# Last stage of a two-layer kernel: three sequences chosen with the attention, one after it, ranks from sums of signs, rows gathered with addition

## The chip, the cores and the metric

The kernel runs on one core of a Trainium2 chip. A core has a matrix engine (TensorE, PE in the profile), a vector engine (VectorE, DVE), an engine for activations (ScalarE, ACT), a general one (GpSimd, POOL) and one that only issues transfers (SyncE, SP). Each works through its own list of instructions in order and waits on semaphores. Transfers (DMA) are issued from the queues of SP, ACT and POOL; gathers by a list of row numbers are issued by POOL. The metric is the device time of one execution in microseconds (us), the median of several runs. Before the change it is 2228.92 us, the median of 3 runs (2227.93 to 2233.76).

## What is computed

Four sequences of 1024 tokens with 256 features go through two layers. The first (windowed attention and a routed feed-forward) and the second layer's attention are untouched. The second feed-forward is a mixture in which each of 8 experts chooses its 128 tokens of each sequence:

```python
gate_logits = jnp.einsum('bnd,de->bne', x, gate_w)
competitive_gates = sinkhorn(gate_logits)      # 8 rounds: normalise over tokens, then over experts
vals, idx = jax.lax.top_k(jnp.swapaxes(competitive_gates, -1, -2), M)   # M = 1024 // 8 = 128
...
routed = x[b_idx, routed_indices]
outputs = jnp.einsum('ebmd,edf->ebmf', routed, experts) * gate_values
routed_back = jnp.zeros_like(x).at[b_idx, routed_indices].set(vals_bmed)
return routed_back                             # the layer adds this to x
```

(`routed` and `outputs` are shortened here.) A token that several experts choose keeps the result that is written last, that of the largest place among the 128 and, at equal places, of the largest expert number; a token that none chooses gets zero.

## The kernel before

A tile is 128 tokens; there are 32 tiles, 8 to a sequence. The residual stream lives in 32 tiles `x_t` in SBUF, 128x256 each.

**The second attention** is one loop of 256 steps (32 tiles `p` by 8 key blocks `k`). In a step PE makes the scores (`one<-q_st,k_st`), takes away the row maxima (`one<-top_st,minus`) and sums the values (`acc<-wide,v_t`); ACT makes the exponentials (L1870). The row maxima of the tile 12 steps ahead are made in the same loop: in each step DVE reduces one 128x1024 block (L1820) and two 128x512 blocks (L1823). For the last 12 steps there is nothing ahead any more, so these reductions end 12 steps before the loop does. When a tile's maxima are complete they go out to DRAM and come back as rows (`tops_d`, `top_st`, L1843 and L1848, on SP). Jobs beside the attention are generators in lists (`outs`, `projects`, `between`, `gating`, `sort`, `aside`), and `some()` takes a piece of each twice a step. `sort` goes on only where another job gave PE something to do, or when `idle` is set. During the attention PE's instructions are held in the order in which they are written.

**From attention to gates.** `put_out` (L1900 to L1926) makes a tile's attention output, `finish` normalises groups of tiles (on POOL, except for the last tile, on DVE), `gate_steps` normalises them again, writes them to DRAM (`xn_d`) and makes the gates. `share_steps` (L1316 to L1330) is the 8 rounds of normalising: a sum over tokens on PE and five small operations on DVE a round, each waiting for the one before.

**Choosing.** Sequences are taken in two groups of two (`GB = 2`). Group 0 is complete at tile 15. `choose_steps` sorts it during the attention: 16 rounds of MAX8 (the eight largest of each row, L1354), FIND_INDEX8 (their places, L1356) and MATCH_REPLACE8 (striking them out, L1360), over 16 rows (sequence and expert) of 1024. Group 1 is sorted after the attention by `choose_halves` in two parts of 8 rounds, with four FIND_INDEX8 at the end of a part (all at L1420), so that the first 64 tokens of each expert can be fetched while the rest are sorted.

**Experts.** `take_rows` (L1477) gathers an expert's token rows from `xn_d` with one POOL instruction for each. `experts_on` (group 0) and `half_experts` (group 1) transpose them on PE, multiply by the expert's weights, scale by the gate on ACT (L1516, L1553) and write to `y_d` on SP (L1520, L1558).

**Ranks and back.** For each token one needs the row of `y_d` that was to be written last, so the largest rank (place plus one, zero where an expert did not choose the token). Group 0: `ranks` scatters places into a DRAM table `rank_d` (16 indirect writes by POOL, L1993), and `read_ranks` reads it back on SP (L1615). Group 1: `ranks_of` makes, for each expert, a 128x1024 comparison of tokens with places (`hot`, by ACT as a sign in the first part at L2270, by DVE as an equality in the second at L2268), which PE sums into ranks. `sources` (L1570 to L1587) turns ranks into row numbers with 11 operations on DVE. `back` gathers the rows with POOL (L1596) into a tile `yr`, an engine adds `x_t` (L1602), and `put_taken` writes the sum to the output (L1609, SP).

The last two tiles' outputs, group 1's `share_steps`, sorting, experts and rows back all come after the attention, in this order; group 0's experts run beside group 1's sorting. A scheduler places the instructions of this part on their engines.

Of the kernel before, what the change touches and what calls it, by code (L numbers as in the profile page):

```python
# [39 lines left out]
def two_layers(  # L40
# [765 lines left out]
    GB = 2  # L806
    GE = GB * E
    TB = S // P
    GT = GB * TB
# [9 lines left out]
    first_slot = fpool.tile([P, 1, E], F32, name="first_slot")  # L819
    nc.vector.tensor_scalar(first_slot, expert_no, float(CAP), -1.0, ALU.mult, ALU.add)  # L820

    place1_i = fpool.tile([P, 1], I32, name="place1_i")
    nc.gpsimd.iota(place1_i, pattern=[[0, 1]], base=1, channel_multiplier=1)
    place1 = fpool.tile([P, 1], F32, name="place1")
    nc.vector.tensor_copy(place1, place1_i)
# [4 lines left out]
    y_d = [fdram.tile([E * CAP + 1, D], F32, name=f"y_d{b}") for b in range(NB)]  # L830

    rank_d = [fdram.tile([S * E, 1], F32, name=f"rank_d{b}") for b in range(GB)]
    none = fpool.tile([P, S * E // P], F32, name="none")
    nc.gpsimd.memset(none, 0.0)
    for b in range(GB):
        nc.gpsimd.dma_start(out=rank_d[b].rearrange("(p n) o -> p (n o)", p=P), in_=none)
    for b in range(NB):
        nc.gpsimd.dma_start(
            out=y_d[b][E * CAP :, :].rearrange("o (p n) -> (o p) n", p=4), in_=none[:4, :]
        )  # L840
# [468 lines left out]
    def share_steps(g: int, bank, lag: int):  # L1309


        mine = gates[:, g * GT : (g + 1) * GT, :]
        by_seq = mine.rearrange("p (b t) e -> p b t e", b=GB)
        for _ in range(8):
            part = small.tile([P, GB, E], F32, tag="part", name="part")
            nc.vector.tensor_reduce(part, by_seq.rearrange("p b t e -> p b e t"), AX.X, ALU.add)  # L1316
            for _ in range(lag):
                yield 0
            ps = bank()
            mm_on(  # L1320
                ps[:, :GE], lhsT=ones1, rhs=part.rearrange("p b e -> p (b e)"),
                start=True, stop=True,
            )
            rc = small.tile([P, GB, 1, E], F32, tag="rc", name="rc")
            nc.vector.reciprocal(rc[:, :, 0, :], ps[:, :GE].rearrange("p (b e) -> p b e", b=GB))
            nc.vector.tensor_tensor(by_seq, by_seq, rc.to_broadcast([P, GB, TB, E]), ALU.mult)
            rsum = small.tile([P, GT, 1], F32, tag="rsum", name="rsum")
            nc.vector.tensor_reduce(rsum[:, :, 0], mine, AX.X, ALU.add)
            nc.vector.reciprocal(rsum, rsum)
            nc.vector.tensor_tensor(mine, mine, rsum.to_broadcast([P, GT, E]), ALU.mult)  # L1330
            yield 1

    def choose_steps(g: int, bank, chosen, after):

        by_tile = gpool.tile([P, TB, GE], F32, tag="by_tile", name="by_tile", bufs=1)
        nc.vector.tensor_copy(
            by_tile.rearrange("p t (b e) -> p t b e", b=GB),
            gates[:, g * GT : (g + 1) * GT, :].rearrange("p (b t) e -> p t b e", b=GB),
        )
        yield 0  # L1340
        cur = gpool.tile([GE, S], F32, tag="cur", name="cur")
        for hf in range(2):
            ps = bank()
            for t in range(TB // 2):
                turn_on(
                    ps[:GE, t * P : (t + 1) * P], by_tile[:, hf * TB // 2 + t, :], ident
                )
            nc.vector.tensor_copy(cur[:, hf * 512 : (hf + 1) * 512], ps[:GE, :])
            yield 1
        top_v = gpool.tile([GE, CAP], F32, tag="top_v", name="top_v", bufs=1)  # L1350
        top_i = gpool.tile([GE, CAP], U32, tag="top_i", name="top_i", bufs=1)
        for k in range(CAP // 8):
            eight = slice(8 * k, 8 * k + 8)
            nc.vector.max(out=top_v[:, eight], in_=cur)  # L1354
            yield 0
            nc.vector.max_index(out=top_i[:, eight], in_max=top_v[:, eight], in_values=cur)  # L1356
            yield 0
            if k < CAP // 8 - 1:
                nxt = gpool.tile([GE, S], F32, tag="cur", name="cur")
                nc.vector.match_replace(  # L1360
                    out=nxt, in_to_replace=top_v[:, eight], in_values=cur, imm_value=-1.0
                )
                cur = nxt
                yield 0
        top_f = gpool.tile([GE, CAP], F32, tag="top_f", name="top_f", bufs=1)
        nc.vector.tensor_copy(top_f, top_i)
        ps = bank()
        turn_on(ps[:, :GE], top_v, ident[:GE, :GE])
        turn_on(ps[:, GE : 2 * GE], top_f, ident[:GE, :GE])
        slot_gate = gpool.tile([P, GE], F32, tag="slot_gate", name="slot_gate", bufs=1)  # L1370
        nc.vector.tensor_copy(slot_gate, ps[:, :GE])
        slot_tok = gpool.tile([P, GE], F32, tag="slot_tok", name="slot_tok", bufs=1)
        nc.vector.tensor_copy(slot_tok, ps[:, GE : 2 * GE])
        slot_row = gpool.tile([P, GE], I32, tag="slot_row", name="slot_row", bufs=1)
        nc.vector.tensor_copy(slot_row, slot_tok)
        chosen[g] = slot_gate, slot_tok, slot_row
        after()
        yield 1
# [3 lines left out]
    def choose_halves(g: int, bank, chosen, after, pool, parts: int = 2):  # L1382

        by_tile = pool.tile([P, TB, 2, GE], F32, tag="by_tile", name="by_tile", bufs=1)
        for n in range(2):
            nc.vector.tensor_copy(
                by_tile[:, :, n].rearrange("p t (b e) -> p t b e", b=GB),  # L1390
                gates[:, g * GT : (g + 1) * GT, :].rearrange("p (b t) e -> p t b e", b=GB),
            )
        yield 0
        cur = pool.tile([P, 4, S], F32, tag="cur", name="cur", bufs=1)
        for hf in range(2):
            ps = bank()
            for t in range(TB // 2):
                nc.tensor.transpose(
                    ps[:32, t * P : (t + 1) * P],
                    by_tile[:, hf * TB // 2 + t].rearrange("p n e -> p (n e)"),  # L1400
                    ident,
                )
# [19 lines left out]
        for k in range(rounds):  # L1422
# [23 lines left out]
            n = GE // parts  # L1446
            for k0, top in enumerate((top_v, top_f)):
                for j in range(part * 4 // parts, (part + 1) * 4 // parts):
                    q = slice(32 * j, 32 * j + 32)
                    for h in range(parts):  # L1450
                        row = 64 * h + 32 * (j % 2) if parts == 2 else 32 * j
                        with ExitStack() as order:
                            if part:
                                order.enter_context(tc.issue_after(newest["ranks"]))
                            mm(
                                ps[row : row + 32, k0 * n : (k0 + 1) * n],
                                lhsT=top[q].rearrange("p a i -> p (a i)"),
                                rhs=ident[q, 32 * j + h : 32 * j + GE : parts],
# [3 lines left out]
            slot_gate = pool.tile([P, n], F32, tag=f"slot_gate{part}", name="slot_gate", bufs=1)  # L1462
            slot_tok = pool.tile([P, n], F32, tag=f"slot_tok{part}", name="slot_tok", bufs=1)
            slot_row = pool.tile([P, n], I32, tag=f"slot_row{part}", name="slot_row", bufs=1)
# [7 lines left out]
    def take_rows(slots, columns, pool):  # L1472

        xgs = []
        for b, n in columns:
            xg = pool.tile([P, D], F32, tag="xg", name="xg", bufs=16)
# [20 lines left out]

    def experts_on(g: int, xgs, pool, w_all):

        slot_gate = chosen[g][0]  # L1500
# [865 lines left out]
```

## Time and profile before

The profiled execution took 2230.59 us; its span, from the first instruction to the last, is 2228.9 us. The stages that the change touches, by the span's clock:

| us | what runs | length | PE busy | DVE busy | POOL busy |
|---|---|---|---|---|---|
| 1303.9 to 1662.2 | attention, twelve tiles' maxima, no choosing beside it | 3 x 119.4 | 347.9 | 275.9 | 86.8 |
| 1662.2 to 1791.4 | the same, with group 0's normalising rounds | 129.2 | 123.6 | 103.8 | 28.9 |
| 1791.4 to 1922.2 | the same, with group 0's sorting | 130.8 | 123.3 | 122.1 | 25.3 |
| 1922.2 to 2038.5 | the last four tiles' maxima, rest of the sorting | 116.3 | 107.0 | 108.9 | 28.3 |
| 2038.5 to 2100.2 | last 12 steps, last tiles' outputs and gates | 61.7 | 48.0 | 15.2 | 39.8 |
| 2100.2 to 2125.5 | group 1's normalising rounds | 25.3 | 7.3 | 16.2 | 15.0 |
| 2125.5 to 2177.8 | group 1's sorting, group 0's experts and rows back | 52.3 | 35.9 | 50.1 | 30.2 |
| 2177.8 to 2228.9 | second half of group 1's experts, rows back, output | 51.1 | 17.5 | 20.1 | 30.4 |

"Busy" is the time in which an engine had an instruction in work. An idle engine costs nothing by itself: what counts is which chain of waits ends last.

### The profile page before, as it was taken

The numbers are of one execution on the slowest core, as the hardware profiler recorded it, in microseconds if no ns is written. First come the engines' busy times: TensorE is split into PE (matmuls) and PEld (weight loads), VectorE is DVE, ScalarE is ACT, GpSimd is POOL, SyncE is SP. The second block draws the span as 40 slices with busy tenths as digits, with TensorE's granted clock in tenths as the row PEclk, the third lists the DMA queues.
The fourth block names the chain that finished last, engine by engine and source line by source line (L and its number), as shares of the span: only waits on it lengthen the run. The fifth ranks groups of instructions, "written<-read, shape, count | busy, mean of one in ns | idle before, by whom it ended". The sixth has DMA issues, their size and how long they took to land.

```text
span 2228.9 us, 50307 instructions
## 1 busy us (share of the span) xinstructions
PE 2056.2 (92%) x19908; PEld 1345.7 (60%) x19908; DVE 1357.5 (61%) x2704; ACT 1002.5 (45%) x1916; POOL 653.0 (29%) x862
## 2 busy tenths in 40 slices
PE   6999989999999999998899999999999999998563
PEld 4777765655788888864455555555555555544341
DVE  6676654522222222244888777878777899996394
ACT  3555542111122222221266676767666566666331
POOL 3656541342000000022331222213131212115546
PEclk9999999999999999998999999999999999999676
DMA  5111105114167666734252313131313113100235
GB/s 148 53 47 47 49 13 202 48 64 139 43 212 236 225 228 210 238 119 108 75 118 52 71 50 77 50 78 50 68 37 82 40 38 70 50 21 12 79 101 171
DMA packets 207016, 212.77 MB, mean 95 GB/s; under 512 B 90024, under 2 KB 166088, under 8 KB 206780
## 3 DMA queue, kind: packets, MB, share of 16 engines
q1 hardware_dynamic: 183996, 169.46, 26.8%
q0 software_dynamic: 11552, 29.72, 4.5%
q10 hardware_dynamic: 11232, 10.37, 1.3%
q8 instruction: 158, 2.59, 0.5%
q14 instruction: 78, 0.64, 0.1%
HBM read 140.70 MB, written 56.96 MB: 89 GB/s over the span
## 4 chain that ended last, share of the span: by engine, by line
PE 33%; DVE 10%; ACT 3%; issue 2%; DMA 1%; POOL 1%; SPq 0%; POOLq 0%; ACTq 0%; DVEq 0%
PE one L86 21%; PE acc L86 9%; DVE tops L1823 3%; DVE tops L1820 2%; PE two L86 2%; ACT wide L1870 1%; PE two L1543 1%; PE misc L82 1%; DVE top_i L1356 1%; DVE cur L1360 0%; DVE top_v L1420 0%; DVE cur L1420 0%; POOL yr L1596 0%; PE two L2273 0%; DVE top_v L1354 0%
## 5 line engine op out<-in xcount | busy, mean ns | idle before, releaser
L1870 ACT ACTIVATE wide<-one 128x512 f32<-128x512 f32 x1024 | 530.0, 602 | 219.3 <-PE one L86 214.5
L1820 DVE TENSOR_REDUCE tops<-two 128x2 f32<-128x1024 f32 x268 | 325.5, 1216 | 72.5 <-PE two L86 65.0
L1823 DVE TENSOR_REDUCE tops<-one 128x1 f32<-128x512 f32 x488 | 312.7, 678 | 14.3 <-PE one L86 14.2
L86 PE MATMUL acc<-wide,v_t 128*32 128x256 f32 x4096 | 279.9, 391 | 2.6 <-ACT wide L1870 2.1
L86 PE MATMUL two<-xbT,w_t 128*128 128x256 f32 (+1 forms) x1280 | 253.6, 356 | 2.5 <-ACT xbT L1167 1.4
L86 PE MATMUL one<-q_st,k_st 64*128 64x512 f32 x1024 | 243.3, 450 | 2.9 <-ACT wide L1870 1.9
L86 PEld LDWEIGHTS two<-xbT,w_t 128*128 128x128 f32 x1280 | 221.6, 190 | 30.0 <-ACT xbT L1167 1.8
L1200 DVE SCALAR_TENSOR_TENSOR glu_b<-two,b_blk,act_b 128x256 f32<-128x256 f32 (+1 forms) x160 | 72.6, 454 | 245.2 <-ACT act_b L1193 245.2
L86 PE MATMUL one<-top_st,minus 64*128 64x512 f32 x1024 | 213.2, 396 | 2.5 <-DMA top_st<-tops_d 2.5
L1193 ACT ACTIVATE act_b<-two,b_blk 128x256 f32<-128x256 f32 (+1 forms) x160 | 72.1, 451 | 295.7 <-DMA ys_d<-yb 149.3
L86 PE MATMUL one<-k_st,q_st 64*128 64x512 f32 x488 | 173.1, 455 | 29.3 <-ACT wide L1870 21.1
L86 PEld LDWEIGHTS acc<-wide,v_t 128*32 128x32 f32 x4096 | 108.0, 110 | 115.1 <-issue 64.2
L86 PEld LDWEIGHTS one<-q_st,k_st 64*128 64x128 f32 x1024 | 104.3, 185 | 96.3 <-ACT wide L1870 40.6
L289 ACT ACTIVATE act<-two,bT 128x512 f32<-128x512 f32 x60 | 41.2, 687 | 265.6 <-PE two L82 262.8
L86 PEld LDWEIGHTS one<-k_st,q_st 64*128 64x128 f32 x488 | 85.7, 184 | 109.2 <-ACT wide L1870 77.7
L86 PE MATMUL acc<-w_t,glu_b 128*128 128x256 f32 x552 | 125.6, 379 | 0.0
L2058 POOL DMA_INDIRECT yr<-ys_d,slot x64 | 61.6, 962 | 215.8 <-DMA ys_d<-yb 80.9
L1250 POOL TENSOR_TENSOR x<-x,sb_b 128x256 f32<-128x256 f32 x32 | 23.2, 726 | 336.4 <-DVE glu_b L1200 336.4
L82 PE MATMUL two<-wide,w_t 128*128 128x512 f32 x256 | 115.1, 603 | 5.4 <-DVE tops L1820 4.7
L619 POOL TENSOR_SCALAR_AFFINE_SELECT pT<-pT 64x512 f32<-64x512 f32 x128 | 84.2, 658 | 111.7 <-ACT pT L609 109.6
L1925 POOL TENSOR_TENSOR y<-y,wide 128x256 f32<-128x256 f32 x32 | 23.3, 731 | 294.3 <-DVE y L1922 250.3
L86 PEld LDWEIGHTS acc<-w_t,glu_b 128*128 128x128 f32 x552 | 101.9, 190 | 12.3
(420 smaller groups left out, 3379.9 us busy)
## 6 DMA issues: line engine op xcount, KB each, us to landing
w_t<-in_L_ffn_rw_dram SPq DMA_DIRECT2D x120, 512.0 KB
halves<-split SPq DMA_DIRECT2D x64, 256.0 KB
q_st<-halves SPq DMA_DIRECT2D x128, 128.0 KB
k_st<-halves SPq DMA_DIRECT2D x256, 64.0 KB
xb<-xs_d SPq DMA_DIRECT2D x31, 256.0 KB
ys_d<-yb ACTq DMA_DIRECT2D x31, 256.0 KB
xs_d<-zeros SPq DMA_DIRECT2D x5, 1536.0 KB
b_t<-in_L_ffn_rb_dram SPq DMA_DIRECT2D x40, 128.0 KB
```

What stands on the lines that cost most here:

```text
L82: return do(*args, **kw)
L86: done = do(*args, **kw)
L289: nc.scalar.activation(act, ps[0], AF.Silu, bias=bT[0][:, f, e : e + 1])
L619: nc.gpsimd.affine_select(out=part, in_=part, compare_op=ALU.is_ge, fill=0.0, base=0, pattern=[[0, 8], [1, WIN]], channel_multiplier=-1,)
L1193: nc.scalar.activation(act[:, :cols], ps[:, ff * cols : (ff + 1) * cols], AF.Silu, bias=b_blk[0][:, f, n : n + 1],)
L1200: nc.vector.scalar_tensor_tensor(glu[:, f, :cols], ps[:, 512 + ff * cols : 512 + (ff + 1) * cols], b_blk[1][:, f, n : n + 1], act[:, :cols ...
L1250: nc.gpsimd.tensor_tensor(x_t[m], x_t[m], sb3_b, ALU.add).ins, newest_glu[0]
L1820: last = nc.vector.tensor_reduce(tops[:, :, j, kk], whole[0], AX.X, ALU.max)
L1823: last = nc.vector.tensor_reduce(tops[:, hh, j, kk : kk + 1], sc[hh], AX.X, ALU.max)
L1870: newest["scalar"] = nc.scalar.activation(pt[:, hh * 512 : (hh + 1) * 512], sc[hh], AF.Exp).ins
L1925: nc.gpsimd.tensor_tensor(y, y, bo_b, ALU.add)
L2058: ga = nc.gpsimd.indirect_dma_start(out=yr[:, :], out_offset=None, in_=ys_d[:, :], in_offset=bass.IndirectOffsetOnAxis(ap=slots[k][:, i : ...
```

## The change

The first group becomes sequences 0 to 2, the second sequence 3 alone (`SEQS`). One function, `choose_parts`, sorts both, in the manner of `choose_halves`: the first group in one part (16 MAX8, 15 MATCH_REPLACE8, 4 FIND_INDEX8 over 32 rows) once tile 23 is finished, at every step of the attention and at both halves of a step in the last 12; the second group in two parts after the attention. The table of ranks in DRAM is gone. Ranks of all experts come from signs on ACT, summed by PE: a row of sums counts the places up to a token, so the difference of neighbours is the token's rank. `sources` takes this difference, times 8, plus the expert's number, by three small matmuls for each tile, and one maximum on DVE gives the row number. For this the rows of `y_d` are ordered by place, then expert, behind 8 rows of zeros. `back` gathers straight onto `x_t` with an addition in the transfer, and `put` writes `x_t` out. Between the normalising rounds of the second group, PE gets the first group's experts and signs, one pair of experts a round.

```diff
-    GB = 2
-    GE = GB * E
     TB = S // P
-    GT = GB * TB
+    SEQS = (range(NB - 1), range(NB - 1, NB))
...
-    y_d = [fdram.tile([E * CAP + 1, D], F32, name=f"y_d{b}") for b in range(NB)]
-    rank_d = [fdram.tile([S * E, 1], F32, name=f"rank_d{b}") for b in range(GB)]
+    y_d = [fdram.tile([(1 + CAP) * E, D], F32, name=f"y_d{b}") for b in range(NB)]
...
-    def choose_steps(g: int, bank, chosen, after):
...
-    def choose_halves(g: int, bank, chosen, after, pool, parts: int = 2):
+    def choose_parts(g: int, bank, after, parts: int):
...
-            xg = pool.tile([P, D], F32, tag="xg", name="xg", bufs=16)
+            xg = pool.tile([P, D], F32, tag="xg", name="xg", bufs=24)
...
-    def back(b: int, t: int, src_row, n: int, adder, rows):
+    def back(b: int, t: int, src_row):
         i = b * TB + t
-        yr = rows.tile([P, D], F32, tag=f"yr{b // GB}", name="yr", bufs=16)
         nc.gpsimd.indirect_dma_start(
-            out=yr[:, :],
+            out=x_t[i][:, :],
             out_offset=None,
             in_=y_d[b][:, :],
-            in_offset=bass.IndirectOffsetOnAxis(ap=src_row[:, n : n + 1], axis=0),
+            in_offset=bass.IndirectOffsetOnAxis(ap=src_row[:, t : t + 1], axis=0),
+            compute_op=ALU.add,
         )
-        adder.tensor_tensor(yr, yr, x_t[i], ALU.add)
-        taken.append((i, yr))
...
-            if i0 + n == GT:
+            if i0 + n == len(SEQS[0]) * TB:
                 gating.append(share_steps(0, misc_bank, 2))
...
-        def ranks():
...
-                sc = nc.gpsimd.indirect_dma_start(
-                    out=rank_d[n // E][:, :],
...
-            yr = pools["yr"].tile([P, D], F32, tag="yr0", name="yr0", bufs=7)
+            yr = pools["yr"].tile(
+                [P, D], F32, tag="yr0", name="yr0", bufs=7 if pools["yr"] is f0pool else 4
+            )
...
-                some(half == 0 and k % 4 == 0)
+                some(half == 0 or s + AHEAD >= NP * KT)
...
+        def signs(ps, less, n: int, col, start: bool, stop: bool):
+            hot = pool.tile([P, S], BF16, tag="hot", name="hot", bufs=3)
+            nc.scalar.activation(hot, place, AF.Sign, bias=less[:, n : n + 1])
+            for hf in range(2):
+                newest["ranks"] = mm(
+                    ps[:, hf * 512 : (hf + 1) * 512],
+                    lhsT=col,
+                    rhs=hot[:, hf * 512 : (hf + 1) * 512],
+                    start=start,
+                    stop=stop,
+                ).ins
+        def sources(rows, mine):
+            ps = one_bank()
+            one = slice(mine.start, mine.start + 1)
+            for t in range(TB):
+                key = ps[:, t * E : (t + 1) * E]
+                mm(key, lhsT=ones1[one], rhs=expert_no[one, 0], start=True, stop=False)
+                for n, unit in enumerate(times_e):
+                    mm(
+                        key,
+                        lhsT=rows[:, t * P + 1 - n : (t + 1) * P + 1 - n],
+                        rhs=unit[mine, mine],
+                        start=False,
+                        stop=(n == 1),
+                    )
+            src_row = gpool.tile([P, TB], I32, tag="src_row", name="src_row")
+            nc.vector.tensor_reduce(
+                src_row, ps[:, : TB * E].rearrange("p (t e) -> p t e", t=TB), AX.X, ALU.max
+            )
+            return src_row
...
-        xgs0 = take_rows(chosen[0], columns, pool)
-        run(share_steps(1, one_bank, 0))
+        xgs0 = take_rows(chosen[0, 0], [(n // E, n) for n in range(n0 * E)], pool)
...
+        for n, _ in enumerate(share_steps(1, one_bank, 0)):
+            if n:
+                next(expert_jobs)
+            if n > 1:
+                next(sign_job)
...
+        for n, _ in enumerate(expert_jobs):
             next(choose)
+            for _ in range(3):
+                if next(sign_job, None) == (next_b + 1) * E + 1:
+                    backs(next_b, rank_jobs(next_b))
+                    next_b += 1
...
+        less = half_less(1, 1)
         xgs = take_rows(chosen[1, 1], columns, pool)
+        for m in range(E // 2):
+            last_signs(1, m, less)
+        nc.scalar.copy(last_sums[:, 1:], rank1)
+        for m in range(0, E // 2, 2):
+            half_experts(1, 1, m, xgs[m : m + 2], pool, w_all)
+        src_row = sources(last_sums, slice(0, E))
+        backs(NB - 1, src_row)
+        put(NB - 1)
```

## The prediction

> **What bounds the kernel now.** I read the windows by stage first, then the chain of waits, then the timelines of DVE and POOL. The windows are cut so that each of the four below holds 32 steps' maxima (32 of the L1820 reductions). Columns: length, then busy time and instruction count of PE, its weight loads, DVE, ACT and POOL.
>
> ```profile
> 1542.80:1662.20 119.40, 115.94 (x1057) 67.12 (x1055) 91.99 (x145) 81.91 (x156) 28.91 (x33) 1.00 0.26 60
> 1662.20:1791.40 129.20, 123.59 (x1081) 71.84 (x1079) 103.78 (x196) 82.30 (x156) 28.92 (x33) 0.97 0.22 55
> 1791.40:1922.20 130.80, 123.27 (x1057) 67.85 (x1055) 122.14 (x191) 82.21 (x156) 25.29 (x30) 0.97 0.22 54
> 1922.20:2038.50 116.30, 106.96 (x943) 58.85 (x939) 108.92 (x173) 77.28 (x148) 28.29 (x33) 0.97 0.09 25
> ```
>
> Without choosing beside it, PE sets the pace (115.9 of 119.4). With group 0's normalising rounds the same work takes 129.2, with its sorting 130.8, where DVE is busy 122.1: 93%, the most of any window of the attention, so I take that as full. So the choosing is not hidden in the attention; it costs time there.
>
> The chain of waits (start, length, who) shows a second loss there: the row maxima of the last tile wait on SP behind the read of the rank table, which waits for POOL's scatters.
>
> ```profile
> 2049.09 3.04 DMA rank_d<-place,at_i
> ...
> 2052.25 0.39 SPq L1615
> ...
> 2052.75 1.82 DMA top_st<-tops_d
> ```
>
> After the attention everything is one chain, with four marks in DVE's timeline: the last maxima, the last tile's output, the first normalising round, the first MAX8 of group 1, and the two lists of rows:
>
> ```profile
> 2035.63 1.23 DVE L1820 TENSOR_REDUCE tops<-two 128x2 f32<-128x1024 f32 x1 [0.84 <-PE two L86]
> ...
> 2084.76 0.26 DVE L1900 RECIPROCAL rec<-misc 128x16 f32<-128x16 f32 x1 [1.55 <-PE misc L82]
> ...
> 2100.22 0.38 DVE L1316 TENSOR_REDUCE part<-gates 128x16 f32<-128x128 f32 x1
> ...
> 2125.51 1.22 DVE L1420 MAX8 top_v<-cur 32x8 f32<-32x1024 f32 x1
> 2126.76 0.08 DVE L1420 MATCH_VALUE_LOAD cur<-top_v,cur 32x8 f32 x1
> 2126.84 1.20 DVE L1420 MATCH_REPLACE8 cur<-top_v,cur 32x1024 f32<-32x1024 f32 x1
> ...
> 2154.32 0.17 DVE L1466 CAST slot_row<-slot_tok 128x8 int32<-128x8 f32 x1
> ...
> 2177.59 0.24 DVE L1466 CAST slot_row<-slot_tok 128x8 int32<-128x8 f32 x1
> ```
>
> Then POOL's timeline: 8 gathers of token rows, the experts, 16 gathers back, one each 1.25 (0.95 and 0.30 of issue), the last landing 3.94 after its start.
>
> ```profile
> 2181.15 2.52 POOL L1477 DMA_INDIRECT xg<-xn_d,slot_row  x1 [2.66 <-PE two L2273]
> 2183.97 0.95 POOL L1477 DMA_INDIRECT xg<-xn_d,slot_row  x1 [0.30 <-issue]
> ...
> 2221.41 1.11 POOL L1596 DMA_INDIRECT yr<-y_d,src_row  x1 [0.30 <-issue]
> ```
>
> **The sum, stage by stage** (the built order of the instructions says what stands behind what; durations are rows of the trace).
>
> **A, up to the last maxima (2036.9 now).** Removed: 129.2 - 119.4 = 9.8 and 130.8 - 119.4 = 11.4. In the fourth window PE has 943 matmuls instead of 1057, since no projection is left; an undisturbed window is 3.5 longer than PE's busy time, so this would be 110.5, and 5.8 are lost (bounds 0, if the window is undisturbed as it is, and 14). Sum 27. Added: the order puts the 8 rounds, the copies and the first pair of the sort into the last 21 steps. DVE: 21/32 x 92.0 = 60.4; a round's six operations are 0.38 + 0.26 + 0.29 + 0.29 + 0.25 + 0.29 = 1.76 at 128 wide; four of them go to 192 wide, at 0.07 per 64 elements (0.22 and 0.29 for the same sum at 64 and 128): 2.04, eight times 16.3; copies and one MAX8/MATCH_REPLACE8 pair 4.7. Together 81.4, at 93% 87; undisturbed these steps take 21/32 x 110.5 = 72.5. That is 15, or 11 without the projection's share of DVE; I take 13 (bounds 5, 18). A = -14 (-22 to -5).
>
> **B, from there to the first round of the second group (63.3 now).** The sorting stands on DVE in front of the last tiles' outputs: two L1823 1.3, 15 MAX8 at 1.25 and 14 MATCH_REPLACE8 at 1.31 make 37.1, four FIND_INDEX8 4.9 (2146.13 to 2150.97), the last tiles' own small operations 7.2 (their rows between 2039 and 2085 added), and some 3 until POOL has tile 28's residual, for which a statistic queued within the sort waits. That is 53.5 to the last tile's reciprocal (L1900), where it is 47.9 now; the row lists and their conversions add 1.6 behind it. B = +7.2 (+2, if small operations overlap and nothing waits, to +12, if PE, held in its written order, stands at a context that DVE delivers 5 late). The SP wait is gone (PE needs the maxima at 2049.5 and gets them at 2054.6, 5.1), but I cost this gain at nothing: DVE's sort takes its place as what is late. Without that cover it is worth the 5.1.
>
> **C, the rounds up to the first MAX8 (25.3 now).** A round is 2.70. PE now has a pair of experts between two rounds' products: 2.17 a pair (from transposes at 2130.51 to 2132.68), two sign products 0.5, the round's own 0.6: 3.3, in six of eight rounds, +3.6; the rounds get 64 wide, -0.28 x 8 = -2.2; the pair in front of the last transposes +0.6. C = +2 (-2 to +8, if the first pair's transposes wait for gathers: these start as now, some 3 before the rounds, and come each 1.25, 2.5 a pair, below 3.3).
>
> **D, to the first list (28.8 now).** The same 8 MAX8, 8 replacements and 4 indices, but two row-number reductions now stand on DVE among them, and each waits for ACT's signs. After the rounds ACT has 11 signs at 1.07 (three in 3.22), 6 copies at 0.55, 12 scalings at 0.42 and 2 copies at 1.0 until sequence 1's ranks: 22.1, and 2 for PE's 24 small products (8 transposes of the same size take 0.60); DVE would be there after 18.2 of sorting, started 4 later: 24.1 against 22.2. With 1 for sequence 0, D = +3 (0 to +8). **E, from list to list (23.3):** the same instructions, 0.
>
> **F, from the second list to the end (51.1 now).** Four gathers instead of eight, and no comparisons on DVE, so I let the first start at once (now it starts 3.4 after the list and takes 2.52). The fourth starts at 4.0 and lands at 7.7 (3.7 is the median landing of a gather back; that of token rows is 2.8). ACT's four signs and the copy of sums (5.5) lie beside. Transposes 0.6, products of both pairs 3.8, scaling 0.8: 12.9; SP's four writes behind the first pair's, 0.6 each, 15.3; landing 2.3, 17.6. The 24 small products and one maximum end at 14 and are hidden; without that cover 2. Then 8 gathers: 7 x 1.25 + 3.94 = 12.7, and 3.1 to the output's end without the adding: 33.4 or so, 33.9 with gaps. F = -17.2 (-21 to -12).
>
> **The gather with addition** is shown by no row. From below: as the plain gather, 0.95 + 0.30. From above: the longest gather of the trace, 2.52 + 0.30. I take 1.25, since issue writes the same list of rows. The Trainium skill speaks against it: "Collectives: The Full Stack", section "The bandwidth ceiling: the fold count and why AG ≠ RS ≠ AR", says that an addition in a transfer costs nothing itself, but needs a second source read, so two read descriptors for one. By that page POOL might write twice as much, an estimate of 2.2 for each gather, and the sum would be some 2226; no run here shows it.
>
> Smaller edits (buffer counts, `yr0` with 4 buffers where at most 3 are in flight, fewer constants, zeros for `y_d`) lie in the first layer's shadow: 0; if four buffers do not suffice, one gather's landing (3.7).
>
> Sum: -14 + 7.2 + 2 + 3 - 17.2 = -19. Against the span of 2228.9 that is **2210**. The profiled execution took 1.7 more than its span, and 1.7 more than the runs' median, so 2210 is also the median to expect.
>
> **Rivals.**
> *The adding gathers are slow, and the kernel gets slower.* POOL has, in order, 16 of them, 4 token gathers, 8, 4, 8. From sequence 0's row numbers (34 after the first round, at 2093.4 + 34) the end then lies 4 x 1.25 + 24g before the second token gathers, and 18 + 7g + 7 behind: 2093.4 + 64 + 31g, once g is over 1.8. It is slower than now from g = 2.31, by over 0.3% from 2.52; at 2.5 the time is 2235, at 2.82 2245. For it: nothing shows g; against: POOL's work is the list.
> *DVE holds PE more than counted.* A +5, B +5, D +3: 2223. For it: 93% busy in the third window and PE's fixed order; against: DVE has 15 of 61.7 in the last steps now.
> *The attention runs free.* A at -22, B +2: 2197. For it: PE bounds the undisturbed windows; against: the rounds' five dependent steps.
>
> **How the numbers follow.** Forecast 0.46 (2200 to 2219), slow gathers 0.25, DVE 0.17, free attention 0.12. A measurement of this kernel can tell about 0.3% from no change: faster is below 2222, slower above 2236. Faster: 0.45 + 0.03 + 0.12 + 0.12 = 0.72; same: 0.01 + 0.05 + 0.04 = 0.10; slower: 0.17 + 0.01 = 0.18. The range, 2194 to 2232, leaves out most of the slow gathers and the best of the last case.
>
> **What would show it.** Windows with 32 L1820 near 119 and 111 up to tile 29; the first round of the second group near 2093; 2.7 to 3.3 a round; 8 gathers each 1.25 at the end, and some 34 from the second list to the end. I am wrong if gathers with addition take over 2, if the last MAX8 of the first group comes later than 50 after the last L1820, or if DVE waits long for ranks.

## The result: no gain, and where the forecast gain went

The changed kernel takes 2234.98 us (median of 11 runs, 2232.02 to 2240.57), the kernel before 2229.19 in the runs beside it (11 runs, 2226.43 to 2234.88): a ratio of 1.0025, interval 1.0013 to 1.0037. Forecast were 2210 and "faster". The profiled execution took 2232.99 with a span of 2231.3.

The stages are cut at the prediction's marks: last maxima, first normalising round of the second group, first MAX8 of that group, first list of rows, second list, end. The marks in DVE's timeline of the changed kernel (start, length, engine, line, operation; in brackets the idle time ahead and what ended it):

```profile
2017.60 1.20 DVE L1722 TENSOR_REDUCE tops<-two 128x2 f32<-128x1024 f32 x1
...
2071.11 0.24 DVE L1802 RECIPROCAL rec<-misc 128x16 f32<-128x16 f32 x1
...
2089.63 0.27 DVE L1305 TENSOR_REDUCE part<-gates 128x8 f32<-128x64 f32 x1
...
2116.60 1.22 DVE L1363 MAX8 top_v<-cur 32x8 f32<-32x1024 f32 x1
...
2128.71 0.22 DVE L2162 TENSOR_REDUCE src_row<-misc 128x8 int32<-128x64 f32 x1 [5.77 <-PE misc L2154]
...
2149.12 0.23 DVE L2162 TENSOR_REDUCE src_row<-acc 128x8 int32<-128x64 f32 x1 [8.73 <-PE acc L2154]
...
2159.77 0.17 DVE L1409 CAST slot_row<-slot_tok 128x4 int32<-128x4 f32 x1
...
2168.56 0.22 DVE L2162 TENSOR_REDUCE src_row<-misc 128x8 int32<-128x64 f32 x1 [8.54 <-PE misc L2154]
...
2191.27 0.17 DVE L1409 CAST slot_row<-slot_tok 128x4 int32<-128x4 f32 x1
...
2211.18 0.23 DVE L2162 TENSOR_REDUCE src_row<-misc 128x8 int32<-128x64 f32 x1 [19.67 <-PE misc L2154]
```

| stage | before | after | difference | forecast (bounds) |
|---|---|---|---|---|
| A, to the end of the last maxima | 2036.9 | 2018.8 | -18.1 | -14 (-22, -5) |
| B, to the first round | 63.3 | 70.8 | +7.5 | +7.2 (+2, +12) |
| C, to the first MAX8 | 25.3 | 27.0 | +1.7 | +2 (-2, +8) |
| D, to the first list | 28.8 | 43.2 | +14.4 | +3 (0, +8) |
| E, to the second list | 23.3 | 31.5 | +8.2 | 0 |
| F, to the end | 51.3 | 40.0 | -11.3 | -17.2 (-21, -12) |

Up to the first MAX8 the forecast holds: A, B and C give -8.9 against -4.8. D, E and F were to give -14.2 and gave +11.3. (F is cut at the list itself here; the prediction's 51.1 starts 0.2 later.) The four lines with `src_row` say where: three times DVE, in the middle of its sort, stood before a maximum of row numbers until PE had made the keys, 5.77 + 8.73 + 8.54 = 23.0 us, and a fourth time at the end.

What PE did before the first of them is in its timeline. Each tile has one product of L2152 and two of L2154, and each product is recorded twice, so that a row of x2 is one product. These are the last three tiles of sequence 0:

```profile
2125.51 0.36 PE L2152 MATMUL misc<-expert_no,ones 1*128 1x8 f32 x2
2125.73 0.59 PE L2154 MATMUL misc<-times_e,sums_to 8*128 8x8 f32 x4
2126.18 0.36 PE L2152 MATMUL misc<-expert_no,ones 1*128 1x8 f32 x2
2126.40 0.99 PE L2154 MATMUL misc<-times_e,sums_to 8*128 8x8 f32 x4
2127.25 0.57 PE L2152 MATMUL misc<-expert_no,ones 1*128 1x8 f32 x2
2127.68 1.00 PE L2154 MATMUL misc<-times_e,sums_to 8*128 8x8 f32 x4
```

A tile takes 0.67 (2125.51 to 2126.18), 0.22 a product. Near 2126.4 the granted clock of PE falls from 1.00 to 0.51, and from there a tile takes 1.28 (with sequence 2, for instance, 2163.26 to 2164.54), 0.43 a product. I call the 24 products of a sequence a train. The four trains take 6.5, 6.3, 9.0 and 8.4 (first start to last end; the second and third from their first pair of L2154). The windows of the stages C to F (columns as in the prediction; the last three are PE's granted clock, the busy share of the DMA engines and GB/s) show whose time that is:

```profile
2089.60:2116.60 27.00, 25.32 (x119) 17.61 (x120) 13.39 (x54) 17.99 (x28) 20.91 (x22) 0.82 0.56 147
2116.60:2159.80 43.20, 40.70 (x216) 28.10 (x215) 28.00 (x40) 26.38 (x36) 21.09 (x15) 0.84 0.50 108
2159.80:2191.30 31.50, 19.14 (x109) 13.74 (x109) 21.98 (x33) 7.03 (x11) 19.84 (x15) 0.62 0.65 148
2191.30:2231.30 40.00, 17.83 (x96) 12.60 (x95) 0.44 (x3) 8.25 (x12) 16.15 (x12) 0.59 0.38 79
```

In D, PE is busy 40.7 of 43.2, DVE only 28.0, about the length that D had (28.8) when DVE alone decided it. The gather with addition, from POOL's timeline: 1.54 and 0.30 of issue, so 1.84, where 1.25 was taken.

```profile
2162.53 1.54 POOL L1511 DMA_INDIRECT x<-y_d,src_row  x1 [0.30 <-issue]
2164.37 0.99 POOL L1420 DMA_INDIRECT xg<-xn_d,slot_row  x1 [0.30 <-issue]
...
2211.80 1.56 POOL L1511 DMA_INDIRECT x<-y_d,src_row  x1 [14.87 <-DVE src_row L2162]
```

### The profile page after: what moved, and what is told of

Its sections match the earlier page's. It is cut to its first block, busy times and chain, and to the rows that moved or that the text cites. A ratio compares the mean times of both kernels' runs of the same rounds, so it can differ in the third digit from the quotient of the medians.

```text
span 2231.3 us, 50565 instructions
## 1 busy us (share of the span) xinstructions
PE 2086.9 (94%) x20098; PEld 1377.6 (62%) x20098; DVE 1327.9 (60%) x2626; ACT 1029.1 (46%) x1941; POOL 639.2 (29%) x832
## 5 line engine op out<-in xcount | busy, mean ns | idle before, releaser
L86 PE MATMUL one<-q_st,k_st 64*128 64x512 f32 x1024 | 238.3, 450 | 2.9 <-ACT wide L1772 1.9
L1827 POOL TENSOR_TENSOR y<-y,wide 128x256 f32<-128x256 f32 x32 | 23.3, 728 | 301.3 <-DVE y L1824 236.0
```

Source lines behind the costliest of these rows:

```text
L86: done = do(*args, **kw)
L1827: nc.gpsimd.tensor_tensor(y, y, bo_b, ALU.add)
```

## The experiments

The runs came in four groups, each on one chip with the kernel before beside it (medians of the kernel before: 2239.54, 2232.64, 2242.78 and 2241.78). Ratios are to that kernel; times are compared within a group, stages across groups only where the table allows it. All stage lengths come from the marks above, "waits" are DVE's three waits for row numbers ahead of the second list.

| group, kernel | median, ratio (interval) | C | D | E | F | waits |
|---|---|---|---|---|---|---|
| 1 plain gathers | 2253.79, 1.0064 (1.0042, 1.0086) | 42.9 | 53.9 | 32.4 | 36.3 | 32.1 |
| 1 trains twice | 2289.85, 1.0222 (1.0192, 1.0252) | 42.1 | 65.9 | 39.7 | 48.7 | 54.1 |
| 1 one product a tile | 2237.95, 0.9983 (0.9967, 0.9999) | 44.4 | 32.8 | 26.8 | 41.4 | 8.1 |
| 1 maxima late | 2266.17, 1.0118 (1.0087, 1.0149) | 43.7 | 44.2 | 22.9 | 62.9 | 0 |
| 2 changed kernel | 2235.11, 1.0009 (0.9998, 1.0021) | 26.9 | 43.2 | 31.5 | 40.2 | 23.1 |
| 2 plain gathers | 2231.70, 0.9993 (0.9982, 1.0003) | 26.9 | 43.2 | 31.5 | 36.6 | 23.1 |
| 2 one product a tile | 2220.13, 0.9942 (0.9928, 0.9956) | 27.0 | 32.4 | 27.4 | 38.7 | 8.3 |
| 2 better | 2213.65, 0.9917 (0.9903, 0.9932) | 26.8 | 32.4 | 28.5 | 33.5 | 9.4 |
| 3 maxima late, writes moved | 2257.64, 1.0067 (1.0045, 1.0090) | 43.8 | 44.2 | 22.9 | 52.7 | 0 |
| 3 experts out of the rounds | 2262.74, 1.0094 (1.0072, 1.0117) | 22.9 | 68.7 | 32.6 | 48.8 | 39.0 |
| 3 wide products | 2257.19, 1.0045 (1.0015, 1.0075) | 44.8 | 47.8 | 29.2 | 40.0 | 22.9 |
| 3 better, second form | 2235.45, 0.9969 (0.9954, 0.9984) | 44.5 | 32.9 | 22.7 | 39.4 | 4.3 |
| 4 changed kernel | 2251.67, 1.0044 (1.0031, 1.0056) | 45.0 | 43.6 | 31.6 | 38.4 | 23.5 |
| 4 maxima late, writes moved | 2262.02, 1.0086 (1.0055, 1.0116) | 42.8 | 44.2 | 22.9 | 52.6 | 0 |
| 4 experts out of the rounds | 2259.64, 1.0078 (1.0052, 1.0104) | 22.4 | 67.9 | 32.4 | 45.9 | 39.7 |
| 4 better, second form | 2232.69, 0.9959 (0.9945, 0.9974) | 44.5 | 32.8 | 22.7 | 39.4 | 4.2 |

**The changed kernel itself** was run again because C was 15 to 17 us longer in all of group 1 than in the first profile.

> The changed kernel as it is, for a comparison on the chip of the runs beside it. In the runs of the first group the normalising rounds of the second group took 42 to 44 us up to the first MAX8 (27.0 in the first profile of the changed kernel), with two rounds of 12 to 15 and 6 to 9 in which DVE and ACT waited for nothing that the trace names. If that belongs to the chip, this run shows it as well where its neighbours do; if it came from those edits, this run has 27. Stages otherwise as before: 43 and 32 up to the two lists, 40 behind.

> The changed kernel beside the three below. D 43.2, E 31.5, F 40 where C is 27; where C is 42 to 45 (the pauses of the fifth and sixth round), D may hold a part of them, and this run shows which.

In group 2, C is 26.9 and D to F as in the first profile, within 0.2. In group 4, C is 45.0 without any edit, so the pause comes with the chip and not from the edits of group 1; D and E stay at 43.6 and 31.6. In DVE's timeline of the changed kernel in group 4:

```profile
2109.93 0.21 DVE L1314 RECIPROCAL rc<-misc 128x8 f32<-128x8 f32 x1 [11.72 <-remote]
2117.11 0.21 DVE L1314 RECIPROCAL rc<-misc 128x8 f32<-128x8 f32 x1 [5.66 <-remote]
```

"Remote" is an end for which the trace has no instruction or transfer. So D and E can be compared between groups 2 and 4, where the changed kernel shows the same within 0.4, and F only within 1.8. The kernel's disadvantage, 1.0009 on one chip and 1.0044 on another, is probably in part this pause; the kernel before has no profile on the second chip, so this is not shown. What the pause is stays open.

**The addition.** Edit: `back` without its last argument, so that the output lacks the residual.

```diff
             in_offset=bass.IndirectOffsetOnAxis(ap=src_row[:, t : t + 1], axis=0),
-            compute_op=ALU.add,
```

> One edit to the changed kernel: the 32 gathers back lose the addition, so the output holds the experts' rows without the residual. A gather should fall from 1.53 + 0.30 to 0.95 + 0.30. Theory W (the 23 us in which DVE waited for the row numbers of sequences 0 to 2, and the late row numbers of sequence 3, made the loss; the addition is a small part): the two lists stay where they are, near 2159.8 and 2191.3; only the last eight gathers get shorter, 7 x 0.59 = 4.1 and 0.6 of the last: the span goes from 2231.3 to 2226 to 2228. Rival G (POOL's list of slow gathers sets the pace of the whole end): POOL has 26 of its gathers behind the first row numbers, 24 x 0.59 = 14 come off, and the span goes below 2220.

> The gathers back without the addition (the output lacks the residual), beside the changed kernel on the same chip. The addition's price: 8 x 0.59 = 4.7 behind the second list, and nothing before it, as the gathers before it wait for row numbers: 4 to 5 us below the changed kernel, ratio to it 0.998. If POOL's list paced the end, 10 or more.

In group 1 it had no changed kernel beside it, its C and D hold pauses, and its trains run at half speed almost from the start (10.0 for the second), so its total tells nothing. In group 2 everything up to the second list is the same to 0.1, F falls from 40.2 to 36.6, and the median by 3.4. POOL's last gathers:

```profile
2214.78 0.94 POOL L1511 DMA_INDIRECT x<-y_d,src_row  x1 [16.14 <-issue]
2216.03 0.95 POOL L1511 DMA_INDIRECT x<-y_d,src_row  x1 [0.30 <-issue]
```

The addition costs 0.59 a gather, and only the last eight are on the path: 7 x 0.59 = 4.1 and 0.5 behind the last one, less 1.0 because the first of them starts 21.7 behind the list (20.7 before), whose reason I did not follow up. POOL's list does not set the pace in this kernel.

**The trains, doubled.** Edit: `for t in [*range(TB), *range(TB)]:` in `sources`.

> One edit to the changed kernel: each train of 24 small products for row numbers is issued twice (the second overwrites the first, the result is the same). Theory W (PE's trains stand in front of DVE's maxima, and these in the sort's order): each train grows by its own length, 6.5 + 6.3 + 9.0 before the second list and 8.5 behind it; the second list moves from 2191.3 to 2211 to 2214, the end to 2255 to 2262. Rival G or H (trains are hidden beside POOL's gathers or the transfers of outputs): at most 3 later, 2234.

The four waits for row numbers, from the view of L2154 (who waited for it: us, times), of this kernel and of the changed one:

```profile
  DVE src_row L2162: 82.4, 4
```

```profile
  DVE src_row L2162: 42.7, 4
```

Beside the changed kernel of group 4, D is 22.3 longer and E 8.2, 30.5 in sum. The three trains ahead of the second list (from their first pair of L2154) take 17.9, 17.2 and 19.1 in place of 6.7, 6.7 and 9.5, 31.3 more: almost nothing of a train is hidden. A doubled train takes more than twice as long, since what is added runs at 0.43 a product, 10.3 for 24. I had added each train's own length, so the growth up to the second list is above the 20 to 23 expected, and the end is above 2255 to 2262 even without the 15 that C is longer. Beside the plain gathers of the same group D is only 12.0 longer, as these hold a pause of ACT and slow trains in D; E is 7.3 longer, and the last row numbers come 28.6 behind the list in place of 19.8.

**One product a tile.** The sums stand twice in one tile, the second time one column on, above a row of ones; a product with 65 rows does what three did.

```diff
-                mm(key, lhsT=ones1[one], rhs=expert_no[one, 0], start=True, stop=False)
-                for n, unit in enumerate(times_e):
-                    mm(key, lhsT=rows[:, t * P + 1 - n : (t + 1) * P + 1 - n],
-                       rhs=unit[mine, mine], start=False, stop=(n == 1))
+                mm(key, lhsT=rows[:, t * P : (t + 1) * P], rhs=times_e, start=True, stop=True)
...
+        def keep_sums(sums, rank):
+            nc.scalar.copy(sums[:E, :], rank)
+            nc.scalar.copy(sums[32 : 32 + E, 1:], rank[:, : S - 1])
```

> One edit to the changed kernel: the sums are kept twice in one tile, the second time one column on, above a row of ones, so that one product for each tile (8 for a sequence, not 24) gives the key; ACT copies twice, 1.0 more for a sequence. Theory W: a train falls from 6.5 to 9.0 down to 1.8 (0.22 a product at the full clock) to 3.5 (0.43 at half of it). DVE's three waits fall from 23.0 to 9 to 14 in sum, the second list comes 9 to 14 earlier (2177 to 2182), the last row numbers at the outputs' landing or 5 earlier, and the span is 2212 to 2220. Rival H (the small products are hidden by what else is late): 2229 to 2232.

> One product for a tile in place of three, beside the changed kernel on the same chip: D 33 (43), E 27 (32), F 41 (40, as the transfers of outputs, not the row numbers, are late there): 14 to 16 us below the changed kernel. Rival: what the first look showed was the chip; then within 4 us of the changed kernel.

PE's timeline, then DVE's, of group 2: the train is 16 records in 1.95, and DVE's waits are 1.89, 1.90 and 4.49.

```profile
2126.72 1.95 PE L2157 MATMUL misc<-times_e,sums_to 65*128 65x8 f32 x16
```

```profile
2128.71 0.22 DVE L2159 TENSOR_REDUCE src_row<-misc 128x8 int32<-128x64 f32 x1 [1.89 <-PE misc L2157]
...
2143.55 0.23 DVE L2159 TENSOR_REDUCE src_row<-acc 128x8 int32<-128x64 f32 x1 [1.90 <-PE acc L2157]
2152.86 0.17 DVE L1409 CAST slot_row<-slot_tok 128x4 int32<-128x4 f32 x1
2160.15 0.23 DVE L2159 TENSOR_REDUCE src_row<-misc 128x8 int32<-128x64 f32 x1 [4.49 <-PE misc L2157]
```

D loses 10.8, E 4.1, F 1.5 (B is 1.3 longer, which I did not follow up); the median falls by 15.0, with nothing changed but the number of products and how their operands are kept (one copy more on ACT). In D, PE is now busy 27.0 of 32.4, at a granted clock of 0.95. In group 2 this one edit makes the kernel 0.58% faster than the kernel before. In group 1, D and E came out the same, 32.8 and 26.8, and with the longer C there it is 0.17% faster (0.01% to 0.33%).

**DVE's order or PE's list?** ACT copies the keys out of PSUM and the maxima go behind the lists, so that none stands in the sort. In the first form output writes also stood ahead of the last experts' outputs on SP, and F was 62.9; the second form puts those of sequences 1 and 2 behind them, and F is 52.7.

```diff
+            keys = pool.tile([P, TB, E], F32, tag="keys", name="keys", bufs=4)
+            nc.scalar.copy(keys.rearrange("p t e -> p (t e)"), ps[:, : TB * E])
...
+            with tc.issue_after(newest["listed"]):
+                nc.vector.tensor_reduce(src_row, keys, AX.X, ALU.max)
```

> One edit to the changed kernel: ACT copies the keys out of PSUM, and DVE's three maxima are placed behind the lists (those of sequences 0 and 1 behind the first, that of 2 behind the second), so that no maximum stands within the sort; the trains of 24 products stay. POOL gets the token gathers of the first list ahead of all gathers back. Theory W1 (DVE's order is what the trains cost): DVE's sort runs without a wait, the lists come near 2146 and 2169, POOL then has 4 token gathers, 16 gathers back, 4 token gathers, 16 gathers back without a pause, 2146 + 2 x 5.0 + 32 x 1.84 = 2215, and the end lies 5 behind: 2218 to 2222. Rival P (PE itself is late, its trains of 22 us stand in front of the experts, and DVE's order costs little): the lists come near 2150 and 2173 but the first list's experts only near 2172, and the end is not before 2226.

> DVE's maxima behind the lists as in the fourth run, with the writes of sequences 1 and 2 behind the last experts' outputs on SP. Theory P (PE's own list is late in D): although no maximum stands in the sort, the first list comes 42 to 45 behind the first MAX8 (43.2 in the changed kernel), since DVE then waits some 13 to 16 for the list's transposes, which stand on PE behind the trains; E falls from 31.5 to 23, and POOL, which has 16 gathers with addition between the two groups of token gathers, gives it back: the end at 2232 to 2240. Theory W1 (DVE's order alone): D 30 to 32.

> Maxima behind the lists, beside the changed kernel on the same chip. Theory P (PE's list): D as in the changed kernel within 2, with 13 to 16 of DVE's wait in front of the list's copy; E 23; end 2 to 8 above the changed kernel, as POOL has 16 gathers with addition between the token gathers. W1 (DVE's order): D 11 or more below the changed kernel.

All three: D 44.2, E 22.9. In group 4, beside the changed kernel's 43.6, the sort runs through, and DVE waits as long in another place, for the list's transposes (DVE's timeline, then PE's):

```profile
2170.93 1.22 DVE L1363 MAX8 top_v<-cur 32x8 f32<-32x1024 f32 x1
2188.08 0.16 DVE L1408 COPY slot_tok<-acc 128x4 f32<-128x4 f32 x1 [15.93 <-PE acc L82]
```

```profile
2178.82 1.00 PE L2156 MATMUL acc<-times_e,sums_to 8*128 8x8 f32 x4
...
2180.69 0.27 PE L82 MATMUL acc<-ident,top_v 32*32 32x4 f32 x4
2180.89 3.32 PE L1453 MATMUL two<-wide,xgT 128*128 128x256 f32 x8
...
2187.78 0.24 PE L82 MATMUL acc<-ident,top_f 32*32 32x4 f32 x8
```

The indices were ready at 2170.9, PE turned them at 2187.8: behind the train that ended at 2179.8, an expert pair and the signs. So in D it is PE's own list that is late, and DVE's order costs nothing there; in E it is DVE's order, for without the maximum E is 22.9, 0.4 less than before the change. The 8.7 gained in E were more than given back in F (52.6 against 38.4), where POOL had 16 gathers with addition between the two groups of token gathers: the second list stood at 2212.5, and its token gathers began at 2225.0. Here POOL's list does set the pace, and the end is 10.4 above the changed kernel's, more than the 2 to 8 expected.

**Work moved into D.** Seven turns of experts and six signs are taken from between the rounds and put in front of the sort.

> The changed kernel with the first group's experts and signs taken out from between the normalising rounds: seven turns of experts and six signs come in one piece behind the rounds, in front of the sort's first steps. Theory P: PE is full in D (40.7 of 43.2), so what is moved there lengthens it by about its own time on PE, 6 pairs at 2.2 and 6 signs at 0.5, 13 to 18, while C falls from 27 to 23 to 25: 10 to 15 us above the changed kernel. Theory W1 (in D only the maxima's waits count): D grows by less than 5.

> Experts and signs taken out of the rounds, beside the changed kernel on the same chip. P: C 23 without pauses, D 13 to 18 longer than the changed kernel's, the end 10 to 15 above it. W1: D less than 5 longer, the end no more than 1 above it. Where the chip makes ACT pause, its pause falls into D here and into C there, and the sum C + D is to be compared: P 9 to 14 more, W1 0 to 1.

ACT paused in both groups here too. The view puts 25.2 and 23.6 in one piece down to "remote", but for most of that time ACT had nothing to do, as the experts stood behind the rounds. In PE's timeline of group 3, the first transposes are done at 2109.4, and PE goes on when ACT has copied them, at 2118.0:

```profile
2108.29 1.11 PE L1436 MATMUL acc<-ident,xg 128*128 128x128 f32 x4
2109.71 1.12 PE L1436 MATMUL misc<-ident,xg 128*128 128x128 f32 x4 [0.30 <-DVE cur L1346]
2118.02 3.58 PE L1453 MATMUL two<-wide,xgT 128*128 128x256 f32 x8 [7.20 <-ACT xgT L1438]
```

So the pause fills the first 7.7 of D in group 3 and the first 6.7 in group 4. From its end to the first list are 61.0 and 61.2, in which PE is busy 59.7 and 59.9. Without the pause, then, D is 17.6 longer than the 43.6 of the changed kernel, at the upper end of P's 13 to 18 and far above W1's 5. C + D as they stand, 90.3 against 88.5 in group 4, hold different pauses; without 6.7 here and 17.4 there they are 83.6 against 71.1, 12.5 more (P 9 to 14, W1 0 to 1). So it is PE that fills D. The rounds without experts take 2.27 each and C is 22.4, so of C's 27.0 some 4.6 are the experts' (3.6 and 0.6 in the forecast).

**Wide products.** Each small product gets 64 moving columns (8 copies) with the same weights: `rhs=unit[mine, :, mine].to_broadcast([E, 8, E])`.

> Each small product of a train gets 64 moving columns (8 copies of the 8; the maximum reads the first copy), and nothing else: eight times the columns, the same weights. If the weights' 128 columns set the price of a product and the thin work lets the granted clock fall, a train keeps 0.22 a product and does not fall to 0.43: trains of 5.3 to 6.5, E 28 to 30, 2 to 5 us below the changed kernel. If the moving columns set the price, trains of 8 or more from the start and 5 to 10 us above it.

PE's timeline, its first train:

```profile
2152.31 0.38 PE L2152 MATMUL misc<-expert_no,ones 1*128 1x64 f32 x2
2152.53 0.60 PE L2154 MATMUL misc<-times_e,sums_to 8*128 8x64 f32 x4
2152.98 0.54 PE L2152 MATMUL misc<-expert_no,ones 1*128 1x64 f32 x2
...
2154.17 0.63 PE L2152 MATMUL misc<-expert_no,ones 1*128 1x64 f32 x2
2154.59 1.06 PE L2154 MATMUL misc<-times_e,sums_to 8*128 8x64 f32 x4
2155.45 0.63 PE L2152 MATMUL misc<-expert_no,ones 1*128 1x64 f32 x2
```

A tile still takes 0.67 (2152.31 to 2152.98) and then 1.28 (2154.17 to 2155.45), so eight times the columns do not change the pace at either clock. But the granted clock falls to 0.50 all the same, in the second train after two tiles (9.7 in all, a sign's products among them): D is 47.8, the three waits 22.9, and no train is as short as was expected if more columns kept the clock up. That the 128 columns of the weights set the price fits, but weights of fewer columns were not tried; and no changed kernel ran in this group, so its total tells nothing. E, 29.2, falls into the range of 28 to 30 expected by luck: the third train, 8.5, started 2.6 before DVE came to its maximum (0.9 in the changed kernel of group 4).

**A kernel that beats both.** One product a tile; for the last sequence DVE copies the sums, half of the last outputs go out on ACT's queue, and the eight gathers are plain, with DVE adding. In the second form sequence 2's maximum also stands behind the second list, with plain gathers for it too.

```diff
+                newest["outputs"] = (nc.scalar if part and h else nc.sync).dma_start(
...
+                nc.vector.tensor_tensor(x_t[b * TB + t], x_t[b * TB + t], yr, ALU.add)
```

> One product for a tile; for the last sequence the sums are copied by DVE, half of the last outputs go out on ACT's queue, and its eight gathers are plain ones with DVE adding. D and E as in the run with one product alone. F: outputs issued from 10.3 behind the list, four on each queue at 0.62 and 2.3 to land, 15.1; gathers 7 x 1.25 + 3.94, adding 0.3, output 3.1: 31, where the changed kernel has 40. In all 22 to 26 us below the changed kernel, and 0.5 to 1% below the kernel before. If the outputs are not what the last gathers wait for, 4 to 5 less.

> As the better kernel, and sequence 2's maximum stands behind the second list, its eight gathers are plain and come after the last token gathers; DVE adds for sequences 2 and 3 at the end. E falls from 28.5 to 23; F stays near 33.5, as the last outputs (17.8 behind the list) and not POOL's 4 + 8 gathers (0.9 + 12 x 1.25 = 15.9) decide: 5 us below the better kernel, 1% below the kernel before. If POOL's list decides, F grows by 2 to 3.

> Cheap trains, sequence 2's maximum behind the second list, plain gathers for sequences 2 and 3, beside the changed kernel on the same chip. D 32.5, E 22.8, F 33.5 without a pause: 88.8 against 114.7, so 24 to 27 below the changed kernel. If POOL's list decides in F (12 gathers and the last outputs), F is 36 and the end 22 to 24 below.

The first form takes 2213.65, 21.5 below the changed kernel beside it and 0.83% below the kernel before: D 32.4, E 28.5, F 33.5 (31 was expected; the gathers start 17.8 behind the list, not 15.1). The second form brings E to 22.7, but F is 39.4 (33.5 expected) in both groups: in group 4 the last train ends 15.6 behind the list (13.8 in the first form), DVE makes the row numbers only 2.7 after it, an end that the view calls "remote", and the first gather back starts 23.8 behind the list. It is 19.0 below the changed kernel of group 4 (24 to 27 expected) and 0.41% below the kernel before. It has not been run on the chip of group 2, so which of the two forms is better stays open.

## Why the prediction was wrong, step by step

Against the forecast, the span is 21.4 longer: A 4.1 less, B and C even, D 11.4, E 8.2 and F 6.1 more.

- **A, B, C** were right in cause and, within their bounds, in size: the undisturbed attention took 119.4 for 32 maxima, and the choosing in its last steps added some 9 where 13 were allowed. The last tile's reciprocal came 52.3 behind the last maxima (53.5 forecast), and 18.5 lie behind it where 15.5 did (1.6 more forecast), two small errors that cancel. With the experts between the rounds C grew by 1.7.
- **D** is the step that failed: "and 2 for PE's 24 small products (8 transposes of the same size take 0.60)". The row of 0.60 holds not eight transposes but four (x4), each recorded once, 0.11 apart; a product of f32 numbers is recorded twice. So 24 products are 48 passes; at 0.11 each they take 5.3 at the full clock, at 0.21 twice that, and the four trains measured 6.3 to 9.0 in place of 2. PE, which I had taken as having room in D, became the one that ends last there: 40.7 of 43.2. With 16 passes in place of 48, D is 32.4, 0.6 from the forecast of 31.8.
- **E** was forecast as unchanged because "the same instructions" stand there. They do, but sequence 2's maximum stands among them too, a wait that I put at nothing: its train starts only when ACT has made eight more signs, and then takes 9.0, so DVE waits 8.54. With one product a tile 4.49 of the wait are left; without the maximum E is 22.9 (23.3 before).
- **F**: the train, "hidden" by the outputs until 17.6, ended 19.9 behind the list; the first gather back started at 20.5. The gathers took 1.84, within the bounds (1.25 to 2.82) but not the value I took: 7 x 0.59 = 4.1. Together 7.0; F was missed by 6.1, as the tail behind the last gather was 0.4 shorter than I had it and the 0.5 for gaps was not needed. The landing of the outputs was well forecast: with one product a tile it is seen at 17.1. But there the first gather back starts only at 19.2, so of the 2.9 by which the gathers were late the train can account for 1.3; the rest is a gap of some 2 between the landing and the first gather, which the trace puts down to nothing but issue.
- **The rivals**: slow gathers with addition were to make the kernel slower from 2.31 on; they took 1.84, below the prediction's estimate of 2.2 too, and did not decide. DVE's 93% in the attention did not hold PE more than counted (A was better than forecast). The attention ran free in part. None of the three named PE after the attention, and that was where most of the forecast gain was lost. I had marked "if DVE waits long for ranks" as a sign of being wrong, but had given it no price.

The Trainium skill, page "TensorE: Matmul & The Clock Gate", section "LDWEIGHTS (loading the stationary operand)", says that a weight load is paid by its columns, however few rows it has. The trace agrees: the loads for 8x128 take 181 ns at the shortest, those for 65x128 take 186, and elsewhere in this kernel a load of 128 columns takes 186 in the mean (`one<-q_st,k_st`), one of 32 columns 110 (`acc<-wide,v_t`). Read beside the transposes' row, whose weights have 128 columns too, it says that a product with 8 rows is no cheaper than a transpose; that each product goes through PE twice is seen only in the count of records.

## What to carry to other kernels

Price a train of small matrix products by its passes (here, with weights of 128 columns, 0.11 each at the full clock and 0.21 at half of it), not by the little that they compute, and count the records in a row before dividing by them. An instruction that waits for another engine, put into an in-order chain such as a sort, hands the whole wait on to what follows; and if the engine that it waits for is itself full, moving the instruction only moves the wait. Here, stacking the operands so that one product does the work of three gained 15.0, and moving the maxima alone made the kernel slower.

## What was not expected of the hardware

- The granted clock fell to half in the middle of a train that kept PE without a gap (1.00 from 2122.1 to 2126.4 in the changed kernel, 0.51 from there to 2128.7): 0.22 a product for the first 1 to 4 us of a train, 0.43 from there on, with 8 and with 64 moving columns. The expert products behind it start at half speed too (3.32 for eight records, 1.89 elsewhere). The same page, section "Part 1: The HAM clock gate", describes the gate as watching how busy PE is; but ahead of this first fall PE was busy in all of the 10.1 before the train, and through the train. (Ahead of the second and third trains it had waited 0.69 and 1.09.) What makes the clock fall stays open.
- A gather with addition into SBUF holds POOL for 1.54 in place of 0.95, for 128 rows of 1 KB.
- In three of the four groups DVE and ACT paused between the rounds, at instructions whose inputs had long been done. In the changed kernel of group 4 DVE paused for 17.4 in two pieces, the first while POOL issued the 24 token gathers, the second until 3.7 behind the last of them; with the experts out of the rounds only ACT paused, for some 7. In group 2 the same gathers ran without any pause. The kernel before was 7 to 10 us slower in the three groups than in group 2. The cause stays open.
